# Forming the residual of a split operand on GpSimd, and pinning the last batch's butterflies, in a fused convolution and Haar-mixing kernel

## The chip, the cores and the metric

The kernel runs on one core of a Trainium2 chip. The metric is the device time of one execution in microseconds; a kernel is run several times, and the median is compared. One more execution is taken with the hardware profiler on; all busy times, waits and timelines below are of that one.

The engines of the core are named as in the profile: PE is TensorE (matmuls), PEld its weight loads, DVE is VectorE, ACT is ScalarE, POOL is GpSimd, SP is SyncE, which here only issues DMAs. L366 is line 366 of the kernel.

## What is computed

Four layers follow each other on x of shape (4, 64, 256, 256). Layers 0, 1 and 3 are long convolutions with a separable kernel per channel; layer 2 goes into a Haar basis, mixes the channels there with a soft threshold, and goes back:

```
conv(x):   k = einsum('ijk,imk->ijmk', hx, hy)[0]      # hx, hy: small sine networks of position
           y = irfft2(rfft2(x, 2L) * rfft2(k, 2L)/2L)[..., :L, :L]
           return y + x * bias[:, None, None]

mix(x):    f1 = haar2d(x)
           acc = 0
           for i in range(2):
               f4 = einsum('bchw,oc->bohw', f1 * v[i], conv_w[i])
               acc += sign(f4) * relu(abs(f4) - tau[i])
           return haar2d(acc, inverse=True) + x

out = conv3(mix(conv1(conv0(x))))
```

Because the kernel of a convolution is an outer product, the kernel below computes it as two products with Toeplitz matrices, one along each axis, in fp32.

## The kernel before

All work is listed as events, each with a time in "ticks", and written out in the order of those times (the table PLACE gives the fraction of a tick for each kind of step). A compiler pass then orders each engine's queue from that listing: among instructions that its own clock takes to be ready, the one written earlier goes first. So an instruction written later can run earlier on its engine, if the pass takes it to be ready sooner. On the chip each engine then works through its queue in that fixed order, and waits at the head of it.

Four batches are staggered. For each batch there are three stages.

- The forward stage (`convolutions`, 64 channels). Each channel is loaded, goes through two convolutions (`first`, `second`: contractions on PE at L253 and L254, a copy by ACT at L267, a sum with the bias term by DVE at L284), and then through one Haar step along rows (`pairs`, L329 and L330) and further row levels for four channels together (`levels`): lengths 128 and 64 on DVE, lengths 32 to 2 on GpSimd (L342 and L343 in both cases; ten GpSimd instructions for four channels). The column transform is one product on PE with a matrix of signs (`down`, L373) in the one-pass format fp32r, so its operand is split in two: ACT rounds it (`split`, L361), an exact rest is formed by subtraction (`rest`, L366), and PE adds the products of both parts. The pair lies in tile sp, of which there is one buffer. `away` (L385) copies the result out, and a DMA stores it.
- The mixing stage (`mixing`, 64 groups of coefficients, one a tick). PE mixes channels (L441), DVE and ACT scale the result (L460, L465), ACT takes magnitude and sign (L469, L472), DVE shrinks by the threshold (L476), restores the sign (L480), and adds both branches into the large tile z (L486).
- The inverse stage (`inverse`, 64 channels). Butterflies on z undo levels of the column transform in place: `halve` is a subtraction (L291) and a combined multiply and subtract (L292); `level` calls it for a level and a quarter ("chunk") of z, `butterfly` for the first. ACT fetches a channel from z (L525), PE undoes rows (L532, L533) and, for the first 16 channels, columns (L546, after a split at L539 and L540), DVE joins the result with what was kept (L554, L557, L558), and the last convolution follows (L253, L254, L267, L284 again). Chunk 0 goes through PE, chunks 1 to 3 through the butterflies.

Batch b+1's forward stage lies beside batch b's mixing stage. Beside the last batch's mixing stage lie final convolutions of earlier batches that were put off for it (loads named v). Each butterfly has a tick, set by `when`; for the last batch (b + 1 == B) those of chunk 1 to 3 are all written in the inverse stage, from its tick `start` on. They depend only on what was added into z, so levels for which all of it has been added can be issued earlier than they are written.

The order of one tick near the change: levels at 0.730, split, rest, down and away at 0.734 of their ticks (down one tick after split and rest), in the inverse stage halves at 0.522, the sum of the last convolution at 0.542, a butterfly at 0.6.

Of the kernel before, what the change touches and what calls it, by code (L numbers as in the profile page):

```python
# [9 lines left out]
F32 = mybir.dt.float32  # L10
F32R = mybir.dt.float32r
AF = mybir.ActivationFunctionType
ALU = mybir.AluOpType
# [3 lines left out]
B, C, S, EMB, ORD = 4, 64, 256, 33, 64  # L17
# [8 lines left out]
PLACE = {  # L26
    "load": 0.714,
    "a0": 1.643,
    "a0 copy": 1.643,
    "y0": 2.571,  # L30
    "y0 sum": 2.571,
    "a1": 3.5,
    "a1 copy": 3.5,
    "y1": 4.429,
# [64 lines left out]
def conv_seq_kernel(ctx, tc, x, fz, fw, bias, decay, haar, haar_row, factors, vt, taut, wmix, out):  # L99
# [14 lines left out]
    nc = tc.nc  # L114
# [126 lines left out]
    def toeplitz(layer, c, name):  # L241

        t = tp.tile([P, 2, S], F32, name=name, tag="toep")
        nc.sync.dma_start(t, ap(pads[layer], c * 2 * ROW, [[1, P], [ROW, 2], [1, S]]))
        return t
# [40 lines left out]

        return [product, residual]

    def halve(even, odd):

        nc.vector.tensor_sub(odd, even, odd)  # L291
        nc.vector.scalar_tensor_tensor(even, even, 2.0, odd, ALU.mult, ALU.subtract)  # L292

    def level(n, chunk, begin=0, count=None):

        count = n if count is None else count
        v = z.rearrange("p n s x c -> p n s (x c)")[:, chunk].rearrange("p (j e s) x -> p j e s x", e=2, s=P // 2 // n)
        halve(v[:, begin : begin + count, 0, 0, :], v[:, begin : begin + count, 1, 0, :])

    def butterfly():  # L300

        v = z.rearrange("p n s (h k) c -> p n s h k c", k=2)
        for h in range(2):
            halve(v[:, :, 0, h, 0, :], v[:, :, 0, h, 1, :])
# [6 lines left out]
    def at(time, run, unit):  # L311
        events.append((time, len(events), run, unit))

    def convolutions(b, ticks, in_parts=(), border=None):
# [48 lines left out]
        def rest(c):  # L363
            w = parts[c]
            t = sd[:, c % 8].rearrange("p e k w -> p e (k w)")
            nc.vector.tensor_tensor(w[:, 1], t, w[:, 0].bitcast(F32), ALU.subtract)  # L366

        def down(c):
            ps = bank(f"pz_{b}_{c}")
# [33 lines left out]
        for n in range(C // 4):  # L403
            end = ticks[4 * n + 3] + 4
            at(after(end, n) + PLACE["levels"], levels(nc.vector, (128,)), n)
            at(after(end + 1, n) + PLACE["levels"], levels(nc.vector, (64,)), n)
            at(after(end + 1, n) + PLACE["levels"], levels(nc.gpsimd, (32, 16, 8, 4, 2)), n)
            for j in range(4):
                c = 4 * n + j
                if c in in_parts:  # L410
                    at(after(end + 3 + j, n) + PLACE["split"], split, c)
                    at(after(end + 3 + j, n) + PLACE["rest"], rest, c)
                at(after(end + 4 + j, n) + PLACE["down"], down, c)
                at(after(end + 4 + j, n) + PLACE["away"], away, c)
# [94 lines left out]
    def inverse(b, start, put_off):  # L509

        st = {}

        def early(c):
            r = mx.tile([P, 2, 2, P], F32, name=f"r_{b}_{c}", tag="f", bufs=3)
            nc.sync.dma_start(r, keep[b][c])
            st[c]["r"] = r

        def sooner(c):
            st[c] = {}
            if c not in put_off:  # L520
                st[c][2] = toeplitz(2, c, f"t2_{b}_{c}")

        def fetch(c):
            a = mx.tile([P, 2, 2, P], F32, name=f"zc_{b}_{c}", tag="mag")
            nc.scalar.copy(a.rearrange("p h k i -> p (h k) i"), z[:, c // 16, :, :, c % 16].rearrange("p i x -> p x i"))  # L525
            st[c]["z"] = a

        def rows(c):
            a = st[c]["z"]
            ps = psm.tile([P, 2, 2, P], F32, name=f"pw_{b}_{c}", tag="mm")  # L530
            for m in range(2):
                nc.tensor.matmul(ps[:, 0, m, :], a[:, 0, m, :], hsinv, start=True, stop=True)  # L532
                nc.tensor.transpose(ps[:, 1, m, :], a[:, 1, m, :], ident)  # L533
            st[c]["pw"] = ps

        def halves(c):
            w = st[c]["w"] = mx.tile([P, 2, 2, 2, P], F32R, name=f"w_{b}_{c}", tag="f4")
            ps = st[c]["pw"]
            nc.scalar.copy(w[:, 0], ps)  # L539
            nc.vector.tensor_tensor(w[:, 1], ps, w[:, 0].bitcast(F32), ALU.subtract)  # L540

        def cols(c):
            ps = psm.tile([P, 2, 2, P], F32, name=f"pu_{b}_{c}", tag="mm")
            flat = "p e m w -> p (e m w)"
            for i in range(2):
                nc.tensor.matmul(  # L546
                    ps.rearrange(flat), hb, st[c]["w"][:, i].rearrange(flat), start=(i == 0), stop=(i == 1)
                )
            st[c]["pw"] = ps

        def join(c):
            ps = st[c]["pw"]
            t = io.tile([P, 2, 2, P], F32, name=f"t_{b}_{c}", tag="res", bufs=BUFS["res"])
            nc.vector.scalar_tensor_tensor(t, st[c]["r"], 0.5, ps, ALU.mult, ALU.add)  # L554
            u = io.tile([P, 2, S], F32, name=f"u_{b}_{c}", tag="y", bufs=BUFS["y"])
            v = u.rearrange("p m (w e) -> p m w e", e=2)
            nc.vector.tensor_add(v[:, :, :, 0], t[:, 0], t[:, 1])  # L557
            nc.vector.tensor_sub(v[:, :, :, 1], t[:, 0], t[:, 1])  # L558
            st[c]["u"] = u

        def aside(c):
            nc.scalar.dma_start(late[b, c], st.pop(c)["u"])

        along = start - groups - 3

        def when(tick, n, chunk, *span):
            at(tick + PLACE["level"], lambda _: level(n, chunk, *span), 0)

        at(along + 11 + PLACE["level"], lambda _: butterfly(), 0)
        for chunk in range(1, 4):  # L570
            turn = start + 16 * (chunk - 1)
            for n in (1, 2, 4, 8):
                when(along + 12 + 3 * chunk if b + 1 < B else turn, n, chunk)
            when(turn + 1, 16, chunk)
            for i in range(2):
                when(turn + 2 + 2 * i, 32, chunk, 16 * i, 16)
            for i in range(4):
                when(turn + 6 + 2 * i, 64, chunk, 16 * i, 16)

        for c in range(C):  # L580
            for name, stage in zip(("sooner", "early", "fetch", "rows"), (sooner, early, fetch, rows)):
                at(start + c + PLACE[name], stage, c)
            turn = start + c
            if c < 16:
                at(start + c + PLACE["halves"], halves, c)
                at(start + c + PLACE["cols"], cols, c)
                turn += 1
            at(turn + PLACE["join"], join, c)
            if c in put_off:
                at(turn + PLACE["aside"], aside, c)  # L590
            else:
                for name, stage in zip(("a3", "a3 copy", "y3", "y3 sum", "out"), last(b, st)):
                    at(turn + PLACE[name], stage, c)

    def last(b, st):
        return [
            *first(b, st, "u", 2, "a3"),
            *second(b, st, "a3", 2, "u", "y3", "co"),
            lambda c: nc.scalar.dma_start(out[b, c].rearrange("(k p) w -> p k w", p=P), st.pop(c)["y3"]),
        ]  # L600
# [41 lines left out]
    start = ready + 3  # L642
    for b in range(B):
# [10 lines left out]
        start = max(end + C, ready + 3)  # L654
# [115 lines left out]
```

## Time and profile before

| | us |
|---|---|
| median of 3 runs (lowest, highest) | 2919.81 (2915.54, 2923.6) |
| the profiled execution | 2913.15 |
| its span, first to last instruction | 2911.3 |
| PE idle over the span | 84.0 |
| GpSimd busy | 329.7 |
| L291 and L292, busy | 122.1 and 122.3 |
| PE's longest wait after the start: L532 for ACT zc L525, at 2676.9 | 3.6 |

A line of a window has the stretch and its length, then for each engine the busy time and the number of instructions, the granted PE clock as a share, the busy share of the DMA engines and GB/s. A line of a timeline has start, duration, engine, line, operation, tiles, shapes and count, and in brackets the idle time of the engine just before and what ended it. A line of a group has count, busy us, mean ns, and idle us before it with what ended most of it. fp32 matmuls count as two instructions.

The stages by time: the first batch's forward stage to 460 us; mixing of batch 0 from 460 to 870, of batch 1 from 1090 to 1530, of batch 2 from 1745 to 2190, of batch 3 from 2400 to 2675; inverse stages between these and from 2675 to the end.

### The profile page before, as it was taken

How to read it: one execution, taken by the hardware profiler on the slowest of the kernel's cores; microseconds unless marked ns; L12 is line 12 of the kernel's file. 1: busy time of each engine (PE TensorE's matmuls, PEld its weight loads, DVE VectorE, ACT ScalarE, POOL GpSimd, SP SyncE). 2: the span in 40 equal slices, each digit the busy share in tenths (PEclk: the TensorE clock that was granted, in tenths of full speed). 3: DMA queues.
4: the chain of work that ended last, by engine and by line, in shares of the span. 5: the costliest groups of instructions: out<-in, count | busy, mean ns of one | idle time of the engine just before them, and what ended most of it. 6: DMA issues, size and time to landing. Idle time of an engine off the chain costs nothing. (4 is left out here: it accounts for less than half of the span.)

```text
span 2911.3 us, 52368 instructions
## 1 busy us (share of the span) xinstructions
PE 2827.3 (97%) x16566; PEld 2551.1 (88%) x16566; DVE 2499.0 (86%) x4263; ACT 2085.2 (72%) x4950; POOL 329.7 (11%) x644
## 2 busy tenths in 40 slices
PE   8999999999999999999999899999999899999999
PEld 6899998888888898998898898998898898887898
DVE  4656558999998679999998679999998779999985
ACT  2333338999995558989985558998986568887554
POOL 0111111121120001221211001121211000000000
PEclk9999999999999999999999999999999999999999
DMA  5878777666676886777677886777777888776676
GB/s 162 256 229 233 231 233 222 205 205 206 197 213 205 268 260 198 214 213 212 208 214 237 253 269 195 214 215 212 208 212 233 262 278 233 235 233 199 208 237 208
DMA packets 599367, 649.77 MB, mean 223 GB/s; under 512 B 48465, under 2 KB 517044, under 8 KB 598964
## 3 DMA queue, kind: packets, MB, share of 16 engines
q1 hardware_dynamic: 519860, 562.09, 65.2%
q10 hardware_dynamic: 79232, 84.34, 8.2%
q8 instruction: 134, 2.20, 0.3%
q14 instruction: 141, 1.16, 0.1%
HBM read 426.77 MB, written 219.48 MB: 222 GB/s over the span
## 5 line engine op out<-in xcount | busy, mean ns | idle before, releaser
L253 PE MATMUL py<-t,a 128*128 128x256 f32 x3072 | 920.9, 382 | 7.5 <-ACT a L267 6.9
L267 ACT COPY a<-pa 128x512 f32<-128x512 f32 x768 | 490.7, 639 | 430.3 <-PE pa L254 390.5
L465 ACT ACTIVATE f<-px,vt 128x64 f32<-128x64 f32 x2816 | 620.2, 408 | 95.9 <-DVE f L460 95.6
L254 PEld LDWEIGHTS py<-t,a 128*128 128x128 f32 x3072 | 584.3, 190 | 79.8
L254 PE MATMUL py<-t,a 128*128 128x128 f32 x3072 | 590.8, 274 | 0.0
L253 PEld LDWEIGHTS py<-t,a 128*128 128x128 f32 x3072 | 496.2, 191 | 47.5 <-ACT a L267 16.8
L441 PE MATMUL px<-wb,f 128*128 128x256 f32 x2048 | 490.4, 381 | 11.1 <-ACT f L465 10.6
L441 PEld LDWEIGHTS px<-wb,f 128*128 128x128 f32 x2048 | 367.7, 190 | 56.4 <-ACT f L465 17.6
L525 ACT COPY zc<-z 128x512 f32<-128x512 f32 x256 | 281.5, 1101 | 170.6 <-PE pw L533 143.6
L343 POOL TENSOR_TENSOR sd<-less 128x128 f32<-128x128 f32 (+4 forms) x320 | 189.3, 592 | 1884.7 <-DVE less L342 1616.8
L469 ACT ACTIVATE mag<-f 128x1024 f32<-128x1024 f32 x256 | 304.1, 1188 | 21.0 <-DVE z L486 20.4
L476 DVE TENSOR_TENSOR mag<-mag,vt 128x1024 f32<-128x1024 f32 x256 | 312.4, 1220 | 4.6 <-ACT mag L469 3.4
L480 DVE SCALAR_TENSOR_TENSOR mag<-mag,f 128x1024 f32<-128x1024 f32 x256 | 312.7, 1222 | 1.1 <-DVE mag L476 0.5
L253 PE MATMUL pa<-t,y 128*128 128x256 f32 x1024 | 308.5, 383 | 4.7 <-DVE y L284 2.9
L253 PE MATMUL pa<-t,x 128*128 128x256 f32 x1024 | 305.7, 380 | 0.0
L366 DVE TENSOR_TENSOR sp<-sd,sp 128x512 fp32r<-128x512 f32 x256 | 179.1, 700 | 135.0 <-ACT sp L361 133.8
L472 ACT ACTIVATE f<-f 128x1024 f32<-128x1024 f32 x256 | 291.4, 1138 | 3.2
L253 PE MATMUL pa<-t,u 128*128 128x256 f32 x772 | 236.0, 388 | 39.2 <-issue 18.9
L284 DVE SCALAR_TENSOR_TENSOR y<-u,bsb,py 128x512 f32<-128x512 f32 x193 | 143.9, 745 | 124.6 <-PE py L254 101.3
L284 DVE SCALAR_TENSOR_TENSOR y<-x,bsb,py 128x512 f32<-128x512 f32 x256 | 189.8, 742 | 42.7 <-PE py L254 41.7
L254 PEld LDWEIGHTS pa<-t,y 128*128 128x128 f32 x1024 | 194.7, 190 | 26.5
L254 PEld LDWEIGHTS pa<-t,x 128*128 128x128 f32 x1024 | 194.6, 190 | 26.3
(72 smaller groups left out, 4450.8 us busy)
## 6 DMA issues: line engine op xcount, KB each, us to landing
t<-pad SPq DMA_DIRECT2D x768, 256.0 KB, 4.0
x<-in_x SPq DMA_DIRECT2D x256, 256.0 KB, 3.8
coef<-co SPq DMA_DIRECT2D x256, 256.0 KB, 3.0
f<-coef SPq DMA_DIRECT2D x256, 256.0 KB, 3.1
r<-keep SPq DMA_DIRECT2D x256, 256.0 KB, 3.7
out_y<-y ACTq DMA_DIRECT2D x256, 256.0 KB, 4.0
keep<-sums SPq DMA_DIRECT2D x256, 128.0 KB, 2.8
keep<-sd SPq DMA_DIRECT2D x256, 128.0 KB, 2.8
```

What stands on the lines that cost most here:

```text
L253: nc.tensor.matmul(ps[:, m, :], src[:, 0, m * P : (m + 1) * P], t[:, ::-1], start=True, stop=False)
L254: nc.tensor.matmul(ps[:, m, P:], src[:, 1, m * P : (m + 1) * P], t[:, : P - 1 : -1], start=False, stop=True)
L267: nc.scalar.copy(a, s["p" + new])
L284: nc.vector.scalar_tensor_tensor(y, s[res], bsb[:, layer, c : c + 1], s["p" + new], ALU.mult, ALU.add)
L343: engine.tensor_tensor(t[:, :, :, half:length], v[..., 0], v[..., 1], ALU.subtract)
L441: nc.tensor.matmul(ps[:, q, h, :], f[:, q, h * P : (h + 1) * P], wb.rearrange("p r n -> p (r n)"), start=True, stop=True,)
L465: nc.scalar.mul(f4[:, j], px[:, j], scale(g, 0)[:, j : j + 1])
L469: nc.scalar.activation(mag, st[g]["f4"], AF.Abs)
L472: nc.scalar.activation(st[g]["f4"], st[g]["f4"], AF.Sign)
L476: nc.vector.tensor_sub(mag, mag, over(g, 1, 16))
L480: nc.vector.scalar_tensor_tensor(mag, mag, 0.0, st[g]["f4"], ALU.max, ALU.mult)
L525: nc.scalar.copy(a.rearrange("p h k i -> p (h k) i"), z[:, c // 16, :, :, c % 16].rearrange("p i x -> p x i"))
```

## The change

The rest of the split operand in the forward stage is formed by GpSimd in place of VectorE. In the last batch, the first instruction of a butterfly that is written at or after the start of the inverse stage gets an order edge to the DVE instruction written just ahead of it: it can't be issued before that one. The edge is one of order in the same queue, without a semaphore. The second instruction of a butterfly depends on the first through its data.

```diff
-    def halve(even, odd):
-
-        nc.vector.tensor_sub(odd, even, odd)
+    def halve(even, odd, stay=False):
+
+        first = nc.vector.tensor_sub(odd, even, odd)
+        if stay:
+            tc.keep_in_program_order(first)
         nc.vector.scalar_tensor_tensor(even, even, 2.0, odd, ALU.mult, ALU.subtract)
 
-    def level(n, chunk, begin=0, count=None):
+    def level(n, chunk, begin=0, count=None, stay=False):
...
-        halve(v[:, begin : begin + count, 0, 0, :], v[:, begin : begin + count, 1, 0, :])
+        halve(v[:, begin : begin + count, 0, 0, :], v[:, begin : begin + count, 1, 0, :], stay)
...
         def rest(c):
             w = parts[c]
             t = sd[:, c % 8].rearrange("p e k w -> p e (k w)")
-            nc.vector.tensor_tensor(w[:, 1], t, w[:, 0].bitcast(F32), ALU.subtract)
+            nc.gpsimd.tensor_tensor(w[:, 1], t, w[:, 0].bitcast(F32), ALU.subtract)
...
         def when(tick, n, chunk, *span):
-            at(tick + PLACE["level"], lambda _: level(n, chunk, *span), 0)
+            at(tick + PLACE["level"], lambda _: level(n, chunk, *span, stay=tick >= start and b + 1 == B), 0)
```

`tc.keep_in_program_order(ins)` looks up the instruction of the same engine that was written last and adds the edge from it to `ins`.

## The prediction

> **What bounds the kernel now.** I read the page's busy rows first, then the windows by stage, then who waits for whom in each stage, and last the timelines around the instruction that moves.
>
> ```profile
> PE 2827.3 (97%) x16566; PEld 2551.1 (88%) x16566; DVE 2499.0 (86%) x4263; ACT 2085.2 (72%) x4950; POOL 329.7 (11%) x644
> DVE  4656558999998679999998679999998779999985
> POOL 0111111121120001221211001121211000000000
> L366 DVE TENSOR_TENSOR sp<-sd,sp 128x512 fp32r<-128x512 f32 x256 | 179.1, 700 | 135.0 <-ACT sp L361 133.8
> ```
>
> TensorE is busy 97% of the span: all its idle time is 2911.3 - 2827.3 = 84 us, and no change that leaves its work alone can gain more. VectorE is at 9 tenths in three blocks of slices and once more near the end. The line that moves, L366, is 179 us of VectorE. The windows by stage (columns: length, then busy us of PE, PEld, DVE, ACT, POOL):
>
> ```profile
> 460.00:870.00 410.00, 401.57 (x2215) 354.24 (x2214) 403.95 (x679) 402.54 (x1212) 77.27 (x120) 1.00 0.68 204
> 1090.00:1530.00 440.00, 437.77 (x2461) 394.25 (x2460) 432.32 (x708) 392.63 (x1097) 88.06 (x140) 1.00 0.70 210
> 1745.00:2190.00 445.00, 442.79 (x2491) 398.89 (x2490) 437.40 (x725) 396.52 (x1109) 87.96 (x140) 1.00 0.71 209
> 2400.00:2675.00 275.00, 264.93 (x1433) 234.75 (x1432) 274.07 (x389) 237.21 (x555) 0.00 (x0) 1.00 0.78 233
> ```
>
> These are the four mixing stages. In the first, PE, DVE and ACT are all within 8.5 us of full; in the second and third PE idles about 2 us and DVE 8 us. In the fourth DVE idles 0.9 us and PE 10: VectorE is the bound there. L366 runs 50, 53 and 53 times in the first three stages (windows of that line) and never in the fourth: the other 100 lie in the first batch's stage, where DVE has room, and in the inverse stages. So part one of the change touches stages where TensorE is already full.
>
> **What the skill says.** "GPSIMD Engine Reference", section 3.1, gives 4497 ns for a two-input fp32 add over 2048 elements on GpSimd, against 2293 on VectorE: by proportion (my estimate) 1.12 us for 512. "SBUF — State Buffer", section "Who interferes with whom", says that a VectorE instruction with two SBUF inputs contends with a GpSimd instruction that reads SBUF, and that the later one waits for the whole of the other; with one SBUF input it doesn't. The trace agrees:
>
> ```profile
> 843.68 0.45 POOL L343 TENSOR_TENSOR sd<-less 128x128 f32<-128x128 f32 x1 [21.71 <-DVE less L342]
> ...
> 843.79 1.42 DVE L480 SCALAR_TENSOR_TENSOR mag<-mag,f 128x1024 f32<-128x1024 f32 x1
> ...
> 612.67 2.72 POOL L343 TENSOR_TENSOR sd<-less 128x128 f32<-128x128 f32 x1 [25.53 <-DVE less L342]
> ...
> 615.38 0.92 DVE L366 TENSOR_TENSOR sp<-sd,sp 128x512 fp32r<-128x512 f32 x1 [0.25 <-ACT sp L361]
> ```
>
> L480 (mean 1.22) took 0.20 longer because a small GpSimd instruction had begun 0.11 us ahead of it, and the same GpSimd instruction, 0.45 when free, took 2.72 where VectorE ran L480 and L291 back to back. "Perfetto Trace Analysis", section "Optimizing Scalar/DVE Operations", warns for this reason that offloading between the two might not help.
>
> **Part one: the rest on GpSimd.** Removed from VectorE: 256 x L366; the next instruction begins 0.60 us after it (1298.96 to 1299.56 in the timeline; 0.68 busy, with some overlap), so 156 x 0.60 = 94 us in the three full stages.
>
> Added to GpSimd: its price isn't in the trace. From the free small ones in the first stage, 0.23 us for 32 elements and 0.29 for 64 (315.97 and 315.07 in the timeline), the step is 1.9 ns an element, so 0.29 + 448 x 1.9 = 1.13 us; from 64 to 128 elements (0.29 to 0.45) it is 2.5, so 1.41. I take 1.15, near the skill's figure; ends 1.05 and 1.4. GpSimd has room: 77 to 88 us busy of 410 to 445 in a mixing stage, plus 53 x 1.15 = 61.
>
> What VectorE gets back. While GpSimd holds the port, VectorE's next two-input instruction waits. The delay measured was the remaining time less about 0.15, so up to 0.9 us of 1.15. If an instruction with a PSUM operand comes next (L284, 0.66 from start to start, L460), only some 0.3 is left. In a mixing stage about 7 in 10 VectorE instructions have two SBUF inputs (L476, L480, L486, L329, L330, the levels, L557/L558, the butterflies): 0.7 x 0.9 + 0.3 x 0.3 = 0.72 us. So 156 x 0.72 = 112 us returned for 94 saved, and the head-of-queue wait for ACT's cast (2.8 and 2.1 us in stages one and two by the waits) goes: a wash, +18 - 7 = +11, with 6 + 8 + 8 us of idle VectorE to hide it. I put +3 on the end. Bounds: -8 (no blocking, and then only the 8.4 us that PE idles in stage one can be won), +26 (0.9 every time).
>
> The new wait. L373 on TensorE waits for the rest, and behind it in TensorE's queue stands everything, the contractions L253 first; the next cast L361 waits for L373 because tile sp has one buffer. GpSimd's queue holds ten level instructions per four channels (L342/L343), and these are stretched by the port:
>
> ```profile
> 1296.57 3.33 POOL L343 TENSOR_TENSOR sd<-less 128x128 f32<-128x128 f32 x1 [27.42 <-DVE less L342]
> ...
> 1303.06 0.21 POOL L343 TENSOR_TENSOR sd<-less 128x8 f32<-128x8 f32 x1
> ...
> 1297.65 0.73 ACT L361 CAST sp<-sd 128x512 fp32r<-128x512 f32 x1
> ...
> 1298.96 0.68 DVE L366 TENSOR_TENSOR sp<-sd,sp 128x512 fp32r<-128x512 f32 x1
> ...
> 1302.75 0.71 PE L373 MATMUL pz<-sp,hbr 128*128 128x512 f32 x2
> ```
>
> The cast ends at 1298.38 and L373 starts at 1302.75: 4.4 us of room. Alone, the rest needs 0.1 + a port wait of 0 to 2.4 + 1.15: hidden. Behind the levels it starts at 1303.27 and ends near 1304.5: 1.75 us late on a full TensorE. Stages two and three have 140/10 = 14 groups each: 28 x 1.75 = 49 us in full. In stage one the room is shorter: at 584 the cast ends at 584.02, L373 starts at 585.71 (1.7 us), the levels run from 581.70 to 587.14: 2.7 us late, and 3.7 with the stage's mean levels (77.27/12 = 6.4 us, begun 2 us ahead of the cast's end); 12 x 3.7 = 44. Full sum 93 us. The compiler orders the queues by its own clock, so some rests will land between level instructions, and L373 may be put later: I take a third, 31, less 6 us of idle that TensorE has there anyway: +25. In the first batch's stage the levels end at 317.1, the rest 1.15 later, and L373 starts at 318.90: hidden. In the inverse stages the room is 6 us and more: hidden.
>
> Neither part issues or moves a DMA, so SP's and ACT's queues keep their order; GpSimd's queue holds none.
>
> **Part two: the pinned butterflies.** Where VectorE is the bound, butterflies of the last batch now run early:
>
> ```profile
> L291 DVE TENSOR_TENSOR z<-z x10: 217/284/1216, 2408.1 to 2574.3; 128x64 f32<-128x64 f32 x4, 128x128 f32<-128x128 f32 x2, 128x256 f32<-128x256 f32 x2, 128x512 f32<-128x512 f32 x1
> ```
>
> With eight L292, and steps of 0.14, 0.20, 0.33, 0.60 and 1.14 us for 64 to 1024 elements, that is 3.36 + 2.89 = 6.25 us, less 0.56 for the four of butterfly(), which isn't pinned: 5.7 us leave a stage that VectorE bounds, and TensorE (10 us idle) follows until ACT's scaled copies (L465, 4.3 us of its waits there) are late next: -5. They return in the last stage (192 of 236 us busy). There, per channel, 1.92 us of other VectorE work and a mean 18.6/13 = 1.43 of butterflies stand beside 3.28 us of TensorE from channel 16 on (the contractions' repeat at 2791 to 2796): nearly full for 13 ticks, and three ticks at each chunk's start carry 2.6 + 2.28 + 2.28. TensorE's idle at 2743 to 2755 (1.32 + 1.98 + 0.72) may shrink in exchange. I put +1 (bounds -3 and +6). Together -4. The wait added is one of order alone: behind a pinned subtraction stand that tick's L554 and L284.
>
> **Sum.** +3 + 25 - 4 = +24. Against the profiled execution's 2913.15 that is 2937; it lies 6.7 us under the median of the runs, 2919.81, so the forecast for a median is 2944. The measurement can't tell less than 0.3% (8.8 us) from no change.
>
> **Rivals.**
> Faster (0.25): the rest never meets the levels in the queue, or L373 sits later in TensorE's order, so nothing is late; VectorE's relief closes 5 us of stage one's 8.4 and some 4 of the 8.7 us that TensorE waits for L558 at 887 to 894, 1550 to 1565 and 2208 to 2223; part two gives 5: -14, 2906. For it: 4.4 us of room in two of three stages. It decides once the rest ends within that room.
> No change (0.17): lateness within TensorE's own idle, the port a wash, part two 0 to -5: 2917.
> Far slower (0.14): every rest stands behind its levels (+93) and the port costs 0.9 each (+10 beyond what those stalls hide): 3020. For it: written order has the levels first in their tick, and 3.33 us for the first level shows how long GpSimd is kept out.
> That GpSimd rounds to fp32r by a slower path would be part of this last case.
>
> **Numbers.** Forecast case 0.44 (2925 to 2970), faster 0.25, none 0.17, far slower 0.14. The range 2902 to 2998 leaves out about a tenth below and a tenth above. Slower by over 0.3%: 0.44 + 0.14 = 0.58; within: 0.17; faster: 0.25.
>
> **What would show it.** A GpSimd row for L366 of about 1.15 us where VectorE is free and 1.5 to 3 in the mixing stages; L480 and L476 with means above 1.22; waits of PE L373 for POOL L366, now 0.3 us in all, at 20 to 40; of the butterflies only the four of butterfly() before 2675. It is wrong if those waits stay under 5 us, or if VectorE's idle in stages two and three grows well over 8 us, for then the port costs less than the rest did.

## The result, and the profile after

The changed kernel takes 3069.53 us (median of 5 runs, 3067.88 to 3075.57); the kernel before took 2915.54 in the same session. The ratio is 1.0532, 95% interval [1.0514, 1.0549]: slower by 154 us. The forecast was 2944, range 2902 to 2998.

The page's busy row and the groups that the prediction spoke of (the two added lines move the numbers: the rest is now L368, its cast L363, its product L375, the shrink L478, the sign L482):

```profile
PE 2879.8 (94%) x16566; PEld 2580.3 (84%) x16566; DVE 2496.9 (81%) x4007; ACT 2090.9 (68%) x4950; POOL 679.8 (22%) x900
L368 POOL TENSOR_TENSOR sp<-sd,sp 128x512 fp32r<-128x512 f32 x256 | 395.3, 1544 | 1182.4 <-ACT sp L363 1156.7
L478 DVE TENSOR_TENSOR mag<-mag,vt 128x1024 f32<-128x1024 f32 x256 | 332.8, 1300 | 20.1 <-ACT mag L471 19.1
```

VectorE executes 256 instructions fewer and is busy for 2496.9 us against 2499.0, so nearly all the time that it saved has come back as longer durations of what is left (L478 1300 ns against 1220, L482 1257 against 1222, and others). The busy row counts time in which two instructions overlap once. So what was saved is less than the 179.1 us of the old line: a run below that leaves the rests out shows 139. TensorE does the same 16566 instructions, but is busy for 52.5 us more, and idles 3073.8 - 2879.8 = 194 us against 84. So the 162 us of span are 110 of waiting and 52 of slower work.

The windows by exact stage (mixing of batches 0, 1, 2 and 3), columns as before:

```profile
457.80:928.10 470.30, 419.59 (x2200) 368.68 (x2199) 410.06 (x631) 405.63 (x1210) 162.59 (x170) 0.95 0.60 177
1138.30:1626.80 488.50, 454.86 (x2446) 401.59 (x2445) 441.78 (x668) 393.67 (x1103) 157.05 (x191) 0.97 0.63 187
1844.50:2333.10 488.60, 454.70 (x2446) 401.34 (x2445) 442.35 (x668) 393.77 (x1103) 155.98 (x191) 0.97 0.64 187
2546.60:2826.20 279.60, 269.62 (x1471) 241.28 (x1470) 276.38 (x384) 242.22 (x567) 0.00 (x0) 1.00 0.80 233
```

And the same first three stages of the kernel before:

```profile
457.30:865.70 408.40, 399.97 (x2204) 352.75 (x2203) 402.06 (x675) 401.75 (x1212) 77.27 (x120) 1.00 0.68 205
1082.90:1525.50 442.60, 440.37 (x2474) 396.56 (x2473) 434.62 (x722) 394.15 (x1106) 88.06 (x140) 1.00 0.70 209
1740.80:2183.30 442.50, 440.29 (x2474) 396.55 (x2473) 434.63 (x722) 394.10 (x1106) 87.96 (x140) 1.00 0.70 209
```

The three mixing stages with rests in them have grown by 61.9, 45.9 and 46.1 us, 154 in all. The granted TensorE clock, 1.00 in all of them before, is 0.95, 0.97 and 0.97. The last mixing stage, which has no rests, is 4.0 us shorter; the last inverse stage is 11.9 longer.

Who waits, from the list of TensorE's waits of the changed kernel (us in total, times, longest):

```profile
PE pz L375 <- POOL sp L368: 89.8, 37, 6.2
PE pa L253 <- DVE y L284: 26.3, 40, 1.7
```

Both were small before: the product's wait for the rest, then on VectorE, was 0.3 us and the second 2.9. One of the 37, from the timeline:

```profile
748.42 0.74 ACT L363 CAST sp<-sd 128x512 fp32r<-128x512 f32 x1
748.44 3.87 POOL L344 TENSOR_TENSOR less<-less 128x128 f32<-128x128 f32 x2
...
752.27 2.84 POOL L345 TENSOR_TENSOR sd<-less 128x64 f32<-128x64 f32 x1
...
756.13 1.26 POOL L368 TENSOR_TENSOR sp<-sd,sp 128x512 fp32r<-128x512 f32 x1
...
757.44 0.80 PE L375 MATMUL pz<-sp,hbr 128*128 128x512 f32 x1 [4.99 <-POOL sp L368]
758.04 1.05 PE L253 MATMUL py<-t,a 128*128 128x256 f32 x2
...
760.84 0.75 DVE L284 SCALAR_TENSOR_TENSOR y<-y,bsb,py 128x512 f32<-128x512 f32 x1 [5.88 <-PE py L254]
```

Read it from the top. The cast is over at 749.16, but the rest stands in GpSimd's queue behind levels that take long beside VectorE's back-to-back work (3.87 us for two small ones, 2.84 for the next), and begins 7 us later. TensorE waits 4.99 us at the head of its queue. Then it is not back at once: a pair of L253 takes 1.05 us there where it took 0.60 at 748.36, and the granted clock is at half:

```profile
755.00:761.80 6.80, 4.36 (x12) 3.71 (x13) 0.96 (x2) 2.77 (x7) 3.67 (x9) 0.50 0.00 0
```

Meanwhile VectorE idles 5.88 us for TensorE's product.

### The profile page after: what moved, and what is told of

Read it like the earlier page. It is cut to its first block, busy times and chain, and to the rows that moved or that the text cites. A ratio compares the mean times of both kernels' runs of the same rounds, so it can differ in the third digit from the quotient of the medians.

```text
span 3073.8 us, 52476 instructions
## 1 busy us (share of the span) xinstructions
PE 2879.8 (94%) x16566; PEld 2580.3 (84%) x16566; DVE 2496.9 (81%) x4007; ACT 2090.9 (68%) x4950; POOL 679.8 (22%) x900
## 5 line engine op out<-in xcount | busy, mean ns | idle before, releaser
L253 PE MATMUL py<-t,a 128*128 128x256 f32 x3072 | 932.7, 386 | 6.8 <-ACT a L267 6.7
L267 ACT COPY a<-pa 128x512 f32<-128x512 f32 x768 | 478.6, 623 | 464.9 <-PE pa L254 426.2
L254 PEld LDWEIGHTS py<-t,a 128*128 128x128 f32 x3072 | 592.9, 193 | 83.4
L368 POOL TENSOR_TENSOR sp<-sd,sp 128x512 fp32r<-128x512 f32 x256 | 395.3, 1544 | 1182.4 <-ACT sp L363 1156.7
L254 PE MATMUL py<-t,a 128*128 128x128 f32 x3072 | 598.4, 277 | 0.0
L253 PEld LDWEIGHTS py<-t,a 128*128 128x128 f32 x3072 | 504.6, 194 | 43.0 <-ACT a L267 14.3
L284 DVE SCALAR_TENSOR_TENSOR y<-y,bsb,py 128x512 f32<-128x512 f32 x256 | 189.9, 742 | 234.4 <-PE py L254 233.8
L478 DVE TENSOR_TENSOR mag<-mag,vt 128x1024 f32<-128x1024 f32 x256 | 332.8, 1300 | 20.1 <-ACT mag L471 19.1
L253 PE MATMUL pa<-t,y 128*128 128x256 f32 x1024 | 322.1, 397 | 27.6 <-DVE y L284 26.3
L482 DVE SCALAR_TENSOR_TENSOR mag<-mag,f 128x1024 f32<-128x1024 f32 x256 | 321.7, 1257 | 5.6 <-ACT f L474 2.5
L471 ACT ACTIVATE mag<-f 128x1024 f32<-128x1024 f32 x256 | 292.8, 1144 | 24.1 <-DVE z L488 22.4
L253 PE MATMUL pa<-t,x 128*128 128x256 f32 x1024 | 305.8, 380 | 0.0
L345 POOL TENSOR_TENSOR sd<-less 128x128 f32<-128x128 f32 (+4 forms) x320 | 161.6, 505 | 581.8 <-DVE less L344 581.8
L375 PE MATMUL pz<-sp,hbr 128*128 128x512 f32 x512 | 196.6, 452 | 91.2 <-POOL sp L368 89.8
L253 PE MATMUL pa<-t,u 128*128 128x256 f32 x772 | 234.3, 385 | 41.1 <-issue 20.5
```

Of the source, the lines that this page charges most:

```text
L253: nc.tensor.matmul(ps[:, m, :], src[:, 0, m * P : (m + 1) * P], t[:, ::-1], start=True, stop=False)
L254: nc.tensor.matmul(ps[:, m, P:], src[:, 1, m * P : (m + 1) * P], t[:, : P - 1 : -1], start=False, stop=True)
L267: nc.scalar.copy(a, s["p" + new])
L284: nc.vector.scalar_tensor_tensor(y, s[res], bsb[:, layer, c : c + 1], s["p" + new], ALU.mult, ALU.add)
L368: nc.gpsimd.tensor_tensor(w[:, 1], t, w[:, 0].bitcast(F32), ALU.subtract)
L471: nc.scalar.activation(mag, st[g]["f4"], AF.Abs)
```

## The experiments

Stage numbers below compare profiles with that of the kernel before. Times of a line are medians, and ratios are to the kernel before on the same chip (2913.84 to 2916.75 us in the sessions).

### The two parts apart

Part two alone (rest on VectorE, butterflies pinned):

```diff
+        first = nc.vector.tensor_sub(odd, even, odd)
+        if stay:
+            tc.keep_in_program_order(first)
```

> Only the pinned butterflies; the rest stays on VectorE. By stages of the changed kernel the last mixing stage is 4 us shorter and the last inverse stage 12 us longer. If that is the pin's doing: +8 us, some 2924, slower by about 0.3%. If the 12 us come from the other part (a shifted start): -4 us, no change. If the prediction's own figure for this part holds: -4 us.

Part one alone (rest on GpSimd, butterflies free):

```diff
-            nc.vector.tensor_tensor(w[:, 1], t, w[:, 0].bitcast(F32), ALU.subtract)
+            nc.gpsimd.tensor_tensor(w[:, 1], t, w[:, 0].bitcast(F32), ALU.subtract)
```

> Only the rest on GpSimd; no pin. The three mixing stages beside a forward stage should be longer by some 62, 46 and 46 us as in the changed kernel: about 3062 to 3070, whatever the pin does. If the two parts disturbed each other, under 3040.

Part two alone: 2922.01 us, ratio 1.0029 [1.0018, 1.0040]; last mixing stage -3.7, last inverse stage +11.8. Part one alone: 3062.66 us, 1.0505 [1.0489, 1.0521]; the mixing stages +59.4, +46.1, +46.8, with the last two stages unchanged. The parts add: 8 + 149 = 157, against 154 to 156 for the whole change. Part one is nearly all of it.

Where part two's 12 us go is seen on VectorE in the last inverse stage. First the kernel before, then part two alone (timelines):

```profile
2689.40 1.22 DVE L291 TENSOR_TENSOR z<-z 128x1024 f32<-128x1024 f32 x1
...
2693.06 1.22 DVE L292 SCALAR_TENSOR_TENSOR z<-z 128x1024 f32<-128x1024 f32 x1
...
2696.72 1.22 DVE L291 TENSOR_TENSOR z<-z 128x1024 f32<-128x1024 f32 x1
```

```profile
2688.86 1.22 DVE L291 TENSOR_TENSOR z<-z 128x1024 f32<-128x1024 f32 x1
...
2690.59 1.22 DVE L294 SCALAR_TENSOR_TENSOR z<-z 128x1024 f32<-128x1024 f32 x1
...
2696.29 0.75 DVE L284 SCALAR_TENSOR_TENSOR y<-u,bsb,py 128x512 f32<-128x512 f32 x1 [0.66 <-PE py L254]
2696.95 1.22 DVE L291 TENSOR_TENSOR z<-z 128x1024 f32<-128x1024 f32 x1
```

Before, the two halves of a butterfly stood in two neighbouring channels, one in each, and two channels took 2696.72 - 2689.40 = 7.32 us. Pinned to the place where it is written, the butterfly lies whole in one channel, that channel's work runs late, and VectorE idles 0.66 us in the other: 8.09 us for two. That is one pair of channels. Over the whole last inverse stage VectorE is busy for 6.8 us more, with the butterflies that have come back (198.3 against 191.5), and its waits for L254 are 5.2 us longer (43.1 against 37.9): together the 12.

### What VectorE's relief is worth, and what GpSimd's work costs it

The rest left out (the second product reads the rounded part again, so that this part of the operand is not computed):

```diff
-            nc.vector.tensor_tensor(w[:, 1], t, w[:, 0].bitcast(F32), ALU.subtract)
+            pass
...
-                        ps.rearrange(flat), hbr, parts[c][:, i].rearrange(flat), start=(i == 0), stop=(i == 1)
+                        ps.rearrange(flat), hbr, parts[c][:, 0].rearrange(flat), start=(i == 0), stop=(i == 1)
```

> Leaves out the rest altogether; the second product of the column transform reads the rounded part again, so TensorE does the same work and no instruction takes L366's place. It shows what freeing VectorE alone is worth. If TensorE bounds the mixing stages: -5 to -15 us (2900 to 2911). If VectorE bounds them: -30 to -90 us.

The rest kept on VectorE, and a GpSimd subtraction of the same size added beside it, whose result nobody reads:

```diff
             nc.vector.tensor_tensor(w[:, 1], t, w[:, 0].bitcast(F32), ALU.subtract)
+            nc.gpsimd.tensor_tensor(idle[:, 0], t, idle[:, 1], ALU.subtract)
```

> The rest stays on VectorE as before; GpSimd forms in addition one difference of 512 fp32 per channel from the same operand into a tile that nobody reads. Nothing waits for it, so only the shared port can cost. Theory port: each of 156 in the mixing stages takes 0.6 to 0.9 us from VectorE, +60 to +120 us. Theory queue (the late product is what costs): 0 to +40 us, VectorE's busy time 100 to 200 us higher all the same.

Without the rest: 2896.05 us, ratio 0.9941 [0.9927, 0.9955], a little more than the 5 to 15 us expected if TensorE bounds those stages. VectorE is busy 139 us less in all:

```profile
PE 2817.5 (97%) x16566; PEld 2545.4 (88%) x16566; DVE 2360.0 (82%) x4007; ACT 2085.4 (72%) x4950; POOL 307.6 (11%) x644
```

The kernel gains 18: 3.6, 5.1 and 5.2 us in the mixing stages and 8.0 in the first inverse stage, of which the next two inverse stages give some 6 back. In this order of the queues, that is the most that moving the rest away could bring.

With the added subtraction: 3091.07 us, 1.0609 [1.0594, 1.0623], beyond what was expected of the port. VectorE's busy time rises from 2499.0 to 2678.5, by 0.70 us for each of the 256 GpSimd instructions, though its own instructions are the same; waiting at a semaphore isn't counted as busy, so this is time in which an instruction had begun and was held off. TensorE's waits, from its list in that run (an added line moves the numbers by one):

```profile
PE pa L254 <- DVE y L285: 74.8, 52, 3.6
PE pz L375 <- DVE sp L367: 33.2, 18, 3.7
```

So GpSimd's work alone makes VectorE's sums and rests late for TensorE. The order of work can't be the reason: sorted by start, TensorE, VectorE and ScalarE run the same operations, tiles and shapes in the same order as in the kernel before. In the compiled queue these subtractions stand four in a row, which is harsher than in the change itself (median 1.34 us, mean 1.52); the run shows the mechanism and its price per instruction, and its total, which has TensorE's clock at 0.984 in it, isn't to be carried over.

### Taking the late product away, in two ways

With room: the product and the copy after it come one tick later, and the pair has a second buffer.

```diff
-            w = parts[c] = mx.tile([P, 2, 2, S], F32R, name=f"sp_{b}_{c}", tag="sp", bufs=1)
+            w = parts[c] = mx.tile([P, 2, 2, S], F32R, name=f"sp_{b}_{c}", tag="sp", bufs=2)
...
-                at(after(end + 4 + j, n) + PLACE["down"], down, c)
-                at(after(end + 4 + j, n) + PLACE["away"], away, c)
-        return after(ticks[-1] + 11, C // 4 - 1)
+                at(after(end + 5 + j, n) + PLACE["down"], down, c)
+                at(after(end + 5 + j, n) + PLACE["away"], away, c)
+        return after(ticks[-1] + 12, C // 4 - 1)
```

> The rest stays on GpSimd, but the second product and the copy that follows it come one step of the schedule later and the rounded parts get a second buffer; butterflies as before the change. Theory A (the loss is the late product: GpSimd's queue delays the rest, and TensorE waits and then runs at half clock): the 89 us of waits of the product for GpSimd fall under 25, the mean clock returns to 0.99 or more, each mixing stage comes within 20 us of the kernel before, and the time is 2915 to 2960. Rival B (the loss is the port: each GpSimd instruction holds VectorE off by about 0.7 us wherever its consumer stands): the waits for GpSimd go but those for VectorE grow by as much, and the time stays over 3030.

With GpSimd's levels written behind the rest of their tick, the room as in the change. The order edge holds only the first of the ten; the subtraction of the same length isn't held, and in the compiled queue it runs ahead of the rest and the other nine behind:

```diff
-            at(after(end + 1, n) + PLACE["levels"], levels(nc.gpsimd, (32, 16, 8, 4, 2)), n)
+            at(after(end + 1, n) + PLACE["levels"] + 0.006, levels(nc.gpsimd, (32, 16, 8, 4, 2)), n)
...
-                    engine.tensor_tensor(place(t, half), v[..., 0], v[..., 1], ALU.add)
+                    ahead = engine.tensor_tensor(place(t, half), v[..., 0], v[..., 1], ALU.add)
+                    if engine is nc.gpsimd and length == 32:
+                        tc.keep_in_program_order(ahead)
```

> The rest stays on GpSimd with one buffer and its product where it was; only GpSimd's block of ten levels is written behind the rest of the same step, so that a rest does not stand behind the block. Theory A (a rest behind the block is what makes the product late): waits of the product for GpSimd fall from 89 to under 30 us, mixing stages gain 20 to 40 us each over the changed kernel, time 2930 to 2990. Rival B (each rest is late by itself, because VectorE's back-to-back work keeps GpSimd off the memory): the waits stay above 60 us and the time over 3040.

Both have the butterflies free, and both end at the same place: 2988.94 us, 1.0255 [1.0241, 1.0269], and 2987.42 us, 1.0247 [1.0233, 1.0261]. Against part one alone (3062.66) they win 74 and 75 us. TensorE's mean clock is back at 0.997 and 0.998. The waits of the product for GpSimd are gone in the first and 16.7 us in the second. In the mixing stages of part one alone, 23 of 152 rests began more than 3 us after their cast; with nine of the ten levels behind them, none.

One rival remains: when the rest leaves VectorE, the compiler's pass orders VectorE's and ScalarE's queues anew, and a worse order could cost time by itself. The traces settle it. The run without the rest, part one alone and the run with the levels behind it run the same operations, tiles and shapes in the same order on TensorE, VectorE and ScalarE (tiles by name, without the numbers of their buffers). They differ only in what GpSimd does: 2896.05 us without a rest, 2987.42 with the rest ahead of nine levels, 3062.66 with the rest as the pass placed it. So 91 us are GpSimd's rests at their best place tried, and 75 more the block of levels ahead of them; the new order, with VectorE's relief, makes nothing slower (2896.05 against 2913.84). In the middle run TensorE waits for (the numbers moved by two again)

```profile
PE pa L253 <- DVE y L284: 49.3, 61, 2.3
PE pz L375 <- POOL sp L368: 16.7, 20, 1.8
```

The first run was expected between 2915 and 2960 if the late product was all; neither theory had it at 2989. Half of the loss is something else, and TensorE's list in the run with room says for whom it waits now:

```profile
PE pa L253 <- DVE y L284: 56.3, 65, 2.3
```

That was 2.9 us before. One of the 65, from that run's timeline:

```profile
1197.17 1.28 POOL L366 TENSOR_TENSOR sp<-sd,sp 128x512 fp32r<-128x512 f32 x1 [5.57 <-ACT sp L361]
...
1198.09 1.45 DVE L476 TENSOR_TENSOR mag<-mag,vt 128x1024 f32<-128x1024 f32 x1 [1.15 <-ACT mag L469]
...
1199.65 1.23 DVE L480 SCALAR_TENSOR_TENSOR mag<-mag,f 128x1024 f32<-128x1024 f32 x1
...
1201.13 0.41 DVE L486 TENSOR_TENSOR z<-mag 128x256 f32<-128x256 f32 x1
...
1201.46 0.74 DVE L284 SCALAR_TENSOR_TENSOR y<-x,bsb,py 128x512 f32<-128x512 f32 x1
...
1202.25 0.70 PE L253 MATMUL pa<-t,y 128*128 128x256 f32 x2 [1.00 <-DVE y L284]
```

VectorE idled 1.15 us for ACT, was then held off by the rest, which ends at 1198.45 (L476 lasts 1.45 in place of 1.22), and went through the queue without a gap; the y sum at its end is 1.00 us late for TensorE. GpSimd's delay is one link in this chain, VectorE's own idle time ahead of it another.

### Does the second half come from GpSimd's instructions?

More runs with the room. First the control, with all rests on VectorE; then GpSimd forming only those of the odd channels:

```diff
+            engine = nc.gpsimd if c % 2 else nc.vector
+            engine.tensor_tensor(w[:, 1], t, w[:, 0].bitcast(F32), ALU.subtract)
```

> The control of the run with room: the same later products and second buffer of the rounded parts, but the rest stays on VectorE. If the 75 us that the run with room still loses come from GpSimd's instructions, this one stays within 6 us of the kernel before (2908 to 2920). If they come from the later products themselves (coefficients that land later, one step more per batch), it lies at 2950 or above.

> With room, GpSimd forms the rest of every odd channel only, VectorE that of the even ones: half the dose. Theory A (each rest on GpSimd sets back VectorE's queue by its delay, with no threshold): half of the 75 us, so 2940 to 2962, and waits of TensorE for the y sums 20 to 35 us against 56. Rival B (slack of some tenths of a microsecond absorbs single delays, only several in one step cost): under 2930.

The control: 2918.90 us, 1.0014 [1.0007, 1.0021]. Room costs 5 us. Half the rests on GpSimd: 2948.96 us, 1.0118 [1.0102, 1.0133]. All of them: 2988.94. So the first half of the rests adds 30 us and the second 40, with waits of TensorE for y sums of 26.7 and 56.3 us. Rival B, that slack takes up single delays, falls: what slack there is takes up little. (Between these three runs the order of VectorE's queue differs too, so the 70 us are not as clean a figure as the 91 above.)

Could the y sum simply be given more time? In this run all rests are on GpSimd, and the first product of the second layer stands behind the mixing product of its tick:

```diff
-    "a1": 3.5,
-    "a1 copy": 3.5,
+    "a1": 3.54,
+    "a1 copy": 3.54,
```

> With room and all rests on GpSimd, the first product of the second layer is placed behind the mixing product of its step, so that the y sum in front of it has the length of a mixing product (about 1.9 us) more. Theory A (the rest of the loss is the y sum that comes 1 to 2 us late for TensorE): the waits for the y sums fall from 56 to under 20 us and the time to 2925 to 2965. Rival B (VectorE, with the delays, is the bound of the mixing stages and only moves the wait): waits of another product for VectorE or ScalarE take their place and the time stays over 2975.

> The control for the slack: the kernel before with only the first product of the second layer placed behind the mixing product. The waits for y sums are 3 us there, so there is nothing to win: within 8 us of the kernel before, 2906 to 2922; more would mean that the place itself costs, and that has to be taken off the run with room and slack.

With room and slack: 2979.42 us, 1.0217 [1.0198, 1.0236], a gain of 9.5 where 24 to 64 were expected of theory A. The list of TensorE's waits in that run shows why:

```profile
PE py L253 <- ACT a L267: 54.1, 57, 3.1
...
PE pa L253 <- DVE y L284: 4.9, 8, 1.0
```

The wait for y sums is gone, and one for ScalarE's copies has taken its place, almost of the same size. Rival B is right in this point: the wait moves. Its time is just met ("over 2975"), and it didn't name ScalarE alone. Why ScalarE's copies came late there was not followed further. The control, the kernel before with that slack: 2910.76 us, 0.9985 [0.9979, 0.9992], so some 3 of the 9.5 us may be the place's own.

### The butterflies pinned less, and the two small edits together

Rest on VectorE; the butterflies of the last batch are kept only behind the last sum of the last mixing:

```diff
-            tc.keep_in_program_order(first)
+            tc.add_manual_dep(
+                first.ins,
+                final[0].ins.name,
+                mybir.DependencyInfo(mybir.DependencyClass.NoSync, mybir.DependencyReason.DATA),
+                reason="behind the last sum",
+            )
...
-                nc.vector.tensor_add(
+                final[0] = nc.vector.tensor_add(
```

> The rest is on VectorE as before. The last batch's butterflies are kept only behind the last sum of the last mixing, and are free among themselves and against the instructions of the inverse. Theory A (the order of the butterflies inside the inverse is what costs the 12 us of the full pin, and the 4 us of the mixing come from keeping them out of it): last mixing stage -3 to -5 us, last inverse stage within 3 us of the kernel before, time 2907 to 2914 where the kernel before has 2914. Rival B (the butterflies cost the inverse their time wherever they come after the mixing: what the mixing gains is paid there): last inverse +4 to +12, time 2914 to 2923.

> The two edits that cost nothing, together: rest on VectorE, the butterflies of the last batch behind the last sum of the last mixing, the first product of the second layer behind the mixing product. If the gains add (about 2 and 3 us against the kernel before): 2908 to 2911 where the kernel before has 2914, ratio about 0.998; if one takes the other's place, 2911 to 2913.

The looser pin: 2911.95 us, 0.9994 [0.9986, 1.0002]; last mixing stage -3.6, last inverse stage +1.3. The stages are as theory A had them, and rival B's +4 to +12 in the inverse falls. Over the whole kernel the gain can't be told from none. The butterflies' time returns to VectorE there as well (197.4 us busy), but its waits for L254 are 33.7 us, fewer than before; TensorE and ScalarE have the order of the full pin, and VectorE's alone is another. With the slack in addition: 2908.61 us, 0.9973 [0.9963, 0.9983], which is 8 us under the kernel before of its session where the two gains had been 2 and 3. This version beats the kernel before by 0.27%, and with it the changed one; it has no part one in it.

## Why the prediction was wrong

The direction was right (slower had 0.58), and so were the places: all three mixing stages with rests, L375 waiting for L368 on TensorE. The size was not: +24 was forecast and +154 came. By steps:

**The price of the rest on GpSimd** was taken as 1.15 us, ends 1.05 and 1.4. The median is 1.278, the mean in the mixing stages 1.67: right within its ends, and inside the 1.5 to 3 foretold for those stages.

**"0.72 us" returned per rest** was near: against the run without the rest, VectorE's busy time in the three mixing stages is 92 us higher in the changed kernel (0.61 for each of 152 rests) and 112 higher with nine levels behind the rest (0.74); the run that adds GpSimd's work alone has 0.70. The "94 saved" was too much: leaving the rests out takes 70 us off VectorE's busy time in these stages. So the exchange, +18 in the prediction, was some +23 by busy time, and its size isn't what failed.

**"I put +3 on the end"** for that exchange was wrong, and measured about 70 (2988.94 with room against 2918.90 for its control), or 73 by the runs of one order of queues (91 less the 18 that the relief brings). Busy times were set against each other as if a microsecond saved on VectorE and one lost there were worth the same. They aren't. Leaving the rests out altogether gains 18 us, since TensorE, not VectorE, ends those stages. The delays arrive at whatever VectorE happens to do, and in the run with room TensorE waits 53 us longer for y sums. VectorE in turn waits longer for TensorE: in that run its list has

```profile
DVE y L284 <- PE py L254: 296.7, 220, 7.8
```

against 169.8 before. The bounds given, -8 to +26, rested on VectorE's total as well, so they were of no help.

**"I take a third, 31, less 6 us ...: +25"** for the late products was the other step that failed. The full sum, 93 us, was worked out from the order in which the levels are written and from how long they last; the waits measured are 89.8, in the mixing stages 44.0, 22.2 and 22.2 where 44, 24.5 and 24.5 had been worked out. Some luck is in that: it is 16 and twice 10 waits in place of 12 and twice 14. The third was a discount for a compiler that might interleave. It mostly did not: in the mixing stages 36 of 40 groups of levels stand whole in GpSimd's queue, and 4 are split by rests into six and four. The profile of before could not tell, for GpSimd had nothing but these levels in its queue there; the discount had no reason but the doubt.

**Left out altogether** was what a wait does to TensorE's clock. The three mixing windows show 19.6, 14.5 and 14.4 us more of busy TensorE, 48.5 in all, for slightly fewer instructions. In the 102.4 us at half clock that lie in these windows TensorE is busy for 87.1; half of that, 44 us, is an estimate of the clock's part, and where the other 5 come from was not followed. "TensorE: Matmul & The Clock Gate", section "What's actually happening", in the Trainium skill states that the array goes to half its clock after an idle window of about 3.4 us, and returns after a busy one. The trace agrees in kind: half clock from 755.0 to 761.8 around the wait of 4.99.

The two losses overlap, so their waits can't just be added: while the product is late, TensorE waits only 26.3 us for y sums; once it isn't, 56.3. By the runs in turn, from 2914: VectorE's relief, in the new order, -18; GpSimd's rests ahead of nine levels +91; the block of levels ahead of them, with the clock, +75; the pin +7 (2922.01 alone: +8).

That ScalarE's queue would "keep" its order did not hold either: the pass ordered VectorE's and ScalarE's queues anew once the rest was gone from VectorE. By the run without the rest this cost nothing.

**Part two**: "-5" in the last mixing stage measured -3.7; "I put +1 (bounds -3 and +6)" for the last inverse stage measured +11.8. The budget of VectorE's time per channel was right on the mean and missed that a pin fixes where in the two channels the halves lie. That the 12 us belong to the order inside the inverse, and not to the butterflies being there at all, is shown by the looser pin, +1.3.

**The rivals.** The "far slower" one had the mechanism, every rest behind its levels, and gave 3020 with a chance of 0.14. It too lacked the clock, and had the port at +10.

The view that would have warned is in the prediction itself: TensorE idle about 2 us of 440 and VectorE 8. With that little slack in both, and each waiting for the other every tick, delays of 0.6 to 0.7 us at any place, one for each rest, aren't all taken up.

## What to carry to other kernels

Work taken off an engine that isn't the last in its stage gains little, while delays put into a chain of engines that wait for each other every tick cost much of their length (here 91 us of the 151 that came back on VectorE, and 177 of 179.5 where the work was only added): price the two by different rates, and try the removal alone first, since it bounds the gain. An operation that goes to another engine joins that engine's queue: count what stands ahead of it as it is written, stretched as it is, and don't discount it without a reason in the profile. A TensorE wait of some microseconds can cost again in clock, as 19 did here; a pin of order should name the one instruction that must come first, and leave the rest free.

## What the runs showed of the hardware

Reading the granted clock of whole executions in windows of half a microsecond, the changed kernel has 19 stretches at half clock, eight of 3.4 us and eleven of 6.8; the kernel before has four, and the run with room five. In the changed kernel all 19 lie at waits of the column product for GpSimd, from 1.9 to 6.2 us; after the first 20 us of the run, no wait of 2.3 us or more is without one, and a wait of 2.2 has none. So a wait shorter than the 3.4 us that the skill gives for an idle window can lower the clock, and the two lengths are one and two such windows. Why a wait of 1.9 us did it and one of 2.2 did not, and which of the two lengths follows, was not settled.

Of the lock that "SBUF — State Buffer", section "Who interferes with whom", describes, these runs give a price: 0.70 us of VectorE's busy time for each added GpSimd subtraction (median 1.34 us), with the order of VectorE's work unchanged. In the other direction the rest on GpSimd, median 1.28, lasted up to 4.43 us, in a stretch in which VectorE ran without a gap.
